# Preparing the next pair's rows in DRAM during the second scan, and putting the stores of the last result between the convolution's rows

## The chip, the cores and the metric

The kernel runs on one core of a Trainium2 chip. The metric is the device time of one execution in microseconds (us); smaller is better. Engine names in the profile are PE (TensorE, with PEld for its weight loads), DVE (VectorE), ACT (ScalarE), POOL (GpSimd) and SP (the engine whose queue issues most transfers). An engine's name with a q (SPq, ACTq) is its sequencer, which issues transfers and waits.

## The reference, cut to what matters

Eight images of 64 channels and 128 x 128 pixels pass through four residual layers in float32:

```python
x = x + _L0_conv_ref(_gn(x), ...)   # deformable convolution, batch norm over all images, relu
x = x + _L1_conv_ref(_gn(x), ...)   # 3x3 convolution
x = x + _L2_conv_ref(_gn(x), ...)   # state-space scan over rows and over columns, mixed by a linear map
x = x + _L3_conv_ref(_gn(x), ...)   # quarter-size image, nearest neighbours, attention, upsampling
```

`_gn` is a group norm: it needs the mean and variance over a whole image of two channels each. The batch norm at the end of layer 0 needs statistics over all eight images, so that layer 0 is finished for every image before its result can be scaled, put through the relu and added to x.

## The kernel before, in words

Two images make a pair, with 2 x 64 channels on the 128 partitions; four pairs are worked through. The deformable layer (the first 14 ms) leaves its raw result of each pair in DRAM, in `self.y[p]`. Everything after it is in `rest`. Two buffers of the size of an image pair, `rooms[0]` and `rooms[1]`, stay in SBUF, and change roles with each pair: `now` (called `a`) holds the running sum x, `other` (called `b`, or `two` in the convolution) holds an intermediate.

For each pair p:

- `conv3x3` scales x by the group norm (`nx`, L574, sixteen steps of 8 rows) and sends each step by four transfers from SP (L576, L577) into `two`, a copy of the image split in even and odd rows. TensorE then multiplies (L588), and VectorE adds into `a` (L590). Between its steps, the nearest-neighbour stage of the pair before (`neighbours`, the generator `aside`) is advanced. That stage begins with `quarter`, which reads `self.y[p]` back from DRAM by transfers from ACT (L1036) and multiplies it (L1022, L1044).
- `scan_layer` normalizes a into b (`first_norm`), and runs two ways, over rows and over columns. A way has a pass back and a pass ahead of 16 blocks each (`NG` is 16). In a round of the pass ahead (`Scan.ahead`) the inputs of a block two rounds on are read from `b` (L1224) and rearranged by transfers from SP (L1226, tile `in`), the states of the pass back are loaded (L1280, tile `zb`), POOL adds and multiplies (L1242, L1286, L1288, L1334), VectorE scans (L1257), TensorE mixes (L1235, L1302, L1320, L1338), and VectorE adds to `a` (L1340). In the second way it also takes statistics of `a` (L1343), two instructions a block. Each round ends with `next(aside)`. The first way's `aside` is the second way's pass back; the second way's `aside` is `following`.
- `following` prepares pair p + 1. It does nothing for `NG - 1` rounds. Then, when `b` is no longer read, it calls `finish_deform`: sixteen chunks of 1024 columns, each with a load of x into `b` (L540), a load of y into a small buffer (L542), the batch norm and relu on ACT (L543), the addition by POOL and VectorE in turn (L544) and two statistics on VectorE (L546). The small buffers are three that stand free: the tiles `inb` and `fx` of the scan, and a slot of `tabs`.
- After `scan_layer`, sixteen stores from SP (L504) write the finished `a` to `self.y[p]`. They are ahead of the next convolution's row transfers in the same queue, and those overwrite the same SBUF buffer.

The code's order is a priority and not the order on the chip: the order of the instructions on each engine is settled when the program is built, and in the profile some instructions of a later step stand well ahead of their place in the code. On the chip each engine runs its list in order and waits at semaphores.

Of the kernel before, what the change touches and what calls it, by code (L numbers as in the profile page):

```python
# [9 lines left out]
F32 = mybir.dt.float32  # L10
I32 = mybir.dt.int32
AF = mybir.ActivationFunctionType
# [4 lines left out]
P = 128  # L17
# [3 lines left out]
CH = 512  # L21
NCH = HW // CH
# [6 lines left out]
NB = 256  # L29
NG = HW // (T * NB)  # L30
# [11 lines left out]
class Net:  # L42
# [434 lines left out]
    def rest(self):  # L477
        tc, nc = self.tc, self.nc
        with ExitStack() as ctx:
            pool = lambda name, bufs, **kw: ctx.enter_context(tc.tile_pool(name=name, bufs=bufs, **kw))  # L480
            self.big = pool("b_big", 1)
            self.small = pool("b_small", 2)
            self.tables = pool("b_tables", 2)
            self.ps = pool("b_ps", 2, space=PSUM)
            self.ps1 = pool("b_ps1", 1, space=PSUM)
            self.back = [[self.dram.tile([P, 2, NB], F32, name=f"back{d}_{g}") for g in range(NG)] for d in range(2)]
            rooms = [self.big.tile([P, ROOM], F32, name=f"room{k}") for k in range(2)]
            image = lambda t: t[:, 0:HW].rearrange("p (h w) -> p h w", h=H)
            aside = iter(())
            with tc.tile_pool(name="b_first", bufs=6) as wp:  # L490
                first = self.finish_deform(0, image(rooms[0]), lambda n: wp.tile([P, 1024], F32, tag="y", name=f"yr0_{n}"))
                for _ in first:
                    pass
            for p in range(self.npair):
                now, other = rooms[p % 2], rooms[(p + 1) % 2]
                a, b = image(now), image(other)
                r, nb = self.conv3x3(p, a, other, *self.gn1, aside)
                norm = self.scan_layer(p, a, b, r, nb)
                af = now[:, 0:HW]

                for n in range(8):
                    for half in range(2):
                        s = slice((half * 8 + n) * 1024, (half * 8 + n + 1) * 1024)
                        nc.sync.dma_start(self.y[p][:, s], af[:, s])  # L504
                aside = self.neighbours(p, self.y[p] if p + 1 < self.npair else af, norm)
            for _ in aside:
                pass

    def setup_deform(self, psum):

# [36 lines left out]
            yield  # L547
        self.gn1 = self.groupnorm(self.small, self.ps1, "small", st, "gn1")

    def conv3x3(self, p, a, room, r, nb, aside):  # L550

# [7 lines left out]
        with self.tc.tile_pool(name=f"b_conv{p}", bufs=1) as cp, self.tc.tile_pool(name=f"b_conv2_{p}", bufs=2) as wp:  # L559
# [3 lines left out]
            for e in range(2):  # L563
                for n in range(2):
                    for h in range(2):
                        dy = 2 * n - 1 + h - e
                        if abs(dy) < 2:
                            nc.scalar.dma_start(w[half[h], e, n], src[:, 3 * dy + 3 : 3 * dy + 6, :])
            nc.gpsimd.memset(two[half[0], :, 0, :], 0.0)
            nc.gpsimd.memset(two[half[1], :, H // 2, :], 0.0)  # L570
            for n in range(16):
                t = wp.tile([P, 2, 4, H], F32, tag="t", name=f"nx{p}_{n}")
                rows = a[:, 8 * n : 8 * n + 8, :].rearrange("p (m e) w -> p e m w", e=2)
                nc.scalar.activation(t, rows, AF.Identity, bias=nb, scale=r)  # L574
                for i in range(2):
                    nc.sync.dma_start(two[half[1], i, 4 * n : 4 * n + 4, :], t[half[i], 0])  # L576
                    nc.sync.dma_start(two[half[0], i, 4 * n + 1 : 4 * n + 5, :], t[half[i], 1])  # L577
            for n in range(0, H // 2, 4):
                for e in range(2):
                    po = self.ps.tile([P, 4, H], F32, tag="b", name=f"c1_{p}_{n}_{e}")  # L580
# [337 lines left out]
    def scan_layer(self, p, a, b, r, nb):  # L918
# [3 lines left out]
        with tc.tile_pool(name=f"b_scan{p}", bufs=2) as wp:  # L922
            ways = [Scan(self, wp, p, d, a, b, st) for d in range(2)]

            back = ways[0].back("in", "z", "h")
            for _ in self.first_norm(wp, p, a, b, r, nb):
                next(back)
                next(back)
            for _ in back:
                pass  # L930
            ways[0].ahead(ways[1].back("inb", "zbk", "fx"))

            def following():

                rooms = [(wp, "inb", [P, 2, 2, NB]), (wp, "fx", [P, 2, 2, NB]), (self.tables, "tabs", [P, NSTATE])]

                def room(n):
                    pool, tag, shape = rooms[n % 3]
                    kind = {"bufs": 1} if pool is wp else {}
                    t = pool.tile(shape, F32, tag=tag, name=f"yr{p + 1}_{n}", **kind)  # L940
                    return t[:, 0:1024] if len(shape) == 2 else t.rearrange("p i h m -> p (i h m)")

                for _ in range(NG - 1):
                    yield
                for n, _ in enumerate(self.finish_deform(p + 1, b, room)):
# [477 lines left out]
```

## Time and profile before

| | us |
|---|---|
| median of three runs (18770.06 to 18828.75) | 18815.32 |
| the profiled execution, its own time | 18647.43 |
| its span in the profile | 18645.6 |
| the deformable layer, up to the first load L540 | 13996.8 |
| the last addition to `a` (L1340) of pairs 0, 1 and 2 ends | 15061.0, 16187.2, 17315.4 |
| the convolution (L588) of pairs 1, 2 and 3 starts | 15103.6, 16229.3, 17357.6 |
| that convolution ends | 15352.0, 16476.4, 17605.6 |

| engine | busy us | share of the span |
|---|---|---|
| PE | 11123.6 | 60% |
| DVE | 11377.5 | 61% |
| POOL | 11000.0 | 59% |
| ACT | 3024.1 | 16% |

The shares are means over stages that differ much. What is of use is the busy time in a short stretch, the waits in it, and the instructions in order of time. The profiled execution was faster than the three runs; a saving found in the profile is therefore taken as a difference, not as a time. Positions such as 15061.0 are microseconds from the span's start.

### The profile page before, as it was taken

To read this page: it belongs to the slowest core of one execution; us is meant where nothing else is said; L and a number is where in the kernel's file an instruction comes from. 1 tells how busy PE (TensorE), PEld (TensorE's weight loads), DVE (VectorE), ACT (ScalarE), POOL (GpSimd) and SP (SyncE) were. 2 spreads that over 40 slices of the span, in tenths; PEclk is the share of its full clock that TensorE was granted. 3 is DMA by queue.
4 is the path that set the end of the run, shared out by engine and by line. 5 is a ranking of instruction groups with operands and counts; after the bars stand their busy time and mean duration, and the time that the engine had idled before them with its cause. 6 is when DMAs were issued, how large, how long until landed. Compare 5 with 4: busy or idle time off the path is not lost. (4 is left out here: it accounts for less than half of the span.)

```text
span 18645.6 us, 118301 instructions
## 1 busy us (share of the span) xinstructions
PE 11123.6 (60%) x31224; PEld 3929.2 (21%) x31224; DVE 11377.5 (61%) x27180; ACT 3024.1 (16%) x5658; POOL 11000.0 (59%) x10484
## 2 busy tenths in 40 slices
PE   6655455545555554445654555555427988889886
PEld 1111111111111111111111111111102434435343
DVE  5566666556665556656665566555664765667566
ACT  1000111001100000010000000000003425334242
POOL 5766766666666666766666676766671413315142
PEclk8777677767777666777776777667658989999898
DMA  4333333333333333333333333333333243422423
GB/s 150 103 100 104 116 113 116 109 112 111 117 111 98 97 94 113 112 113 110 100 95 100 93 99 99 99 96 93 92 92 94 69 144 79 130 87 70 142 76 101
DMA packets 900049, 1933.33 MB, mean 104 GB/s; under 512 B 199852, under 2 KB 435764, under 8 KB 876340
## 3 DMA queue, kind: packets, MB, share of 16 engines
q0 software_dynamic: 442368, 1208.55, 21.7%
q1 hardware_dynamic: 381968, 679.49, 11.9%
q10 hardware_dynamic: 75044, 37.72, 1.0%
q8 instruction: 255, 4.18, 0.1%
q14 instruction: 414, 3.39, 0.1%
HBM read 1540.72 MB, written 208.10 MB: 94 GB/s over the span
## 5 line engine op out<-in xcount | busy, mean ns | idle before, releaser
L371 POOL DMA_INDIRECT g<-table,idx x9216 | 9526.3, 1034 | 4333.7 <-issue 2626.2
L381 DVE TENSOR_REDUCE sm<-g 128x64 f32<-128x256 f32 x9216 | 5062.9, 580 | 3356.0 <-remote 2479.9
L289 PE MATMUL po<-xe,wt 128*54 128x512 f32 (+3 forms) x8384 | 4668.4, 666 | 534.0 <-ACT ob L299 390.9
L380 DVE TENSOR_TENSOR g<-g,wts 128x256 f32<-128x256 f32 x9216 | 3561.8, 415 | 552.9 <-DMA g<-table,idx 488.5
L387 PE MATMUL sp<-ident,sm 128*128 128x128 f32 x4096 | 1494.5, 375 | 3632.2 <-DVE sm L381 1853.0
L390 ACT COPY s<-sp 128x512 f32<-128x512 f32 x1024 | 598.1, 584 | 9537.5 <-remote 3918.3
L387 PEld LDWEIGHTS sp<-ident,sm 128*128 128x128 f32 x4096 | 619.5, 155 | 6387.2 <-DVE sm L381 2381.4
L395 PE MATMUL yp<-s,wd 128*64 128x512 f32 (+1 forms) x2560 | 933.0, 736 | 1367.3 <-ACT s L390 756.3
L289 PEld LDWEIGHTS po<-xe,wt 128*54 128x54 f32 x8384 | 916.4, 138 | 1863.7 <-issue 1192.8
L872 POOL COPY l_yb<-ln_y 128x512 f32<-128x512 f32 x128 | 72.8, 612 | 1295.9 <-DVE ln_y L121 1295.9
L588 PE MATMUL c<-room,l_w 128*64 128x508 f32 (+1 forms) x3072 | 741.8, 597 | 22.2 <-DMA room<-nx 16.1
L1242 POOL TENSOR_TENSOR u<-u,v 128x512 f32<-128x512 f32 x256 | 327.9, 1281 | 680.0 <-DVE v L1241 548.8
L1224 ACT ACTIVATE fx<-room,ln_b,ln_g 128x512 f32<-128x512 f32 x512 | 639.2, 1292 | 169.9 <-DMA in<-fx 148.1
L1334 POOL TENSOR_TENSOR ms<-ms,ln_y 128x512 f32<-128x512 f32 x256 | 274.0, 1090 | 640.2 <-DVE ln_y L121 600.3
L389 PE MATMUL s<-ident,sm 128*64 128x128 f32 x1024 | 343.5, 335 | 449.7 <-DVE sm L381 151.2
L396 DVE BATCH_NORM_STATS2 ystat<-yp 128x6 f32<-128x512 f32 x128 | 89.3, 697 | 844.2 <-PE yp L395 498.7
L395 PEld LDWEIGHTS yp<-s,wd 128*64 128x64 f32 (+1 forms) x2560 | 222.9, 161 | 1810.2 <-issue 1000.3
L1257 DVE TENSOR_TENSOR_SCAN z<-tabs,z,u 128x256 f32<-128x256 f32 x512 | 435.4, 876 | 214.8 <-POOL u L1242 186.2
L1235 PE MATMUL pv<-in,tabs 128*128 128x512 f32 x1024 | 506.4, 617 | 41.9 <-DVE u L1241 40.0
L1320 PE MATMUL pc<-outs,h 128*128 128x256 f32 x2048 | 497.7, 386 | 28.0 <-DVE h L1305 25.8
L1302 PE MATMUL py<-x,outs 128*128 128x512 f32 x1024 | 507.3, 599 | 6.8 <-POOL x L1288 6.4
L1302 PE MATMUL py<-in,outs 128*128 128x512 f32 x1024 | 507.3, 608 | 1.7 <-ACT h L1304 1.0
(414 smaller groups left out, 10197.6 us busy)
## 6 DMA issues: line engine op xcount, KB each, us to landing
g<-table,idx POOLq DMA_INDIRECT x9216
in<-fx SPq DMA_DIRECT2D x1024, 128.0 KB
xe<-in_x_dram SPq DMA_DIRECT2D x56, 1408.0 KB
table<-q SPq DMA_DIRECT2D x256, 256.0 KB
y<-ys SPq DMA_DIRECT2D x128, 256.0 KB
room<-in_x_dram SPq DMA_DIRECT2D x64, 512.0 KB
yr<-y SPq DMA_DIRECT2D x64, 512.0 KB
room<-nx SPq DMA_DIRECT2D x256, 128.0 KB
```

Of the source, the lines that this page charges most:

```text
L289: nc.tensor.matmul(po[:, r0:r1, c0:c1], lhsT=wt[:, t, :], rhs=xe[:, row + r0 : row + r1, c0 + dx : c1 + dx], start=n == 0, stop=n == len(u ...
L371: nc.gpsimd.indirect_dma_start(out=tq[:, k, :], out_offset=None, in_=flat[i], in_offset=bass.IndirectOffsetOnAxis(ap=idx[:, at : at + 1], ...
L380: nc.vector.tensor_mul(t[:, k], t[:, k], w)
L381: nc.vector.tensor_reduce(sm[:, k], t[:, k].rearrange("p q c -> p c q"), axis=mybir.AxisListType.X, op=ALU.add)
L387: nc.tensor.transpose(sp[:, j, :], sm[:, j * P : (j + 1) * P], self.ident)
L390: nc.scalar.copy(st[i][:, 0:4, m * P : (m + 1) * P], sp)
L395: nc.tensor.matmul(yp[i * C : (i + 1) * C, :], lhsT=wd[0:rows, j, :], rhs=st[i][0:rows, j, :], start=j == 0, stop=j == 4)
L588: nc.tensor.matmul(o, lhsT=lt, rhs=mv, start=k < 2, stop=k >= len(calls) - 2)
L1224: nc.scalar.activation(fx[:, e].rearrange("p h (o m) -> p h o m", m=self.INNER), src[:, e::2], AF.Identity, bias=w["ln1_b"], scale=w["ln1_g"])
L1235: nc.tensor.matmul(pv, lhsT=tabs[:, at : at + P], rhs=fx[:, :, h, :], start=h == 0, stop=h == 1)
L1302: nc.tensor.matmul(py, lhsT=lt, rhs=mv, start=n == 0, stop=n == len(calls) - 1)
L1320: nc.tensor.matmul(pc[:, i], lhsT=hs[:, h, i, m * P : (m + 1) * P], rhs=self.outs[:, CEN : MIX + P], start=True, stop=True)
```

## The change

`following` now starts at the first round of the second way ahead. It takes one buffer for x (`inb`) and one for y (the slot of `tabs`), and a new function, `prepare_deform`, does in each round one chunk: load x, load y, relu on ACT, addition on POOL (all sixteen), two statistics on VectorE, and a store of the sum to `self.y[p + 1]` in DRAM. The sixteenth chunk and the group norm's few steps follow in round sixteen. Then eight loads of 2048 columns (1 MB each) bring the finished rows from DRAM into `b`. The stores of pair p's result are a generator, `stores`, which `conv3x3` advances: two steps (four stores of 512 KB) ahead of its row steps, and one step (two stores) after every second row step.

```diff
-                r, nb = self.conv3x3(p, a, other, *self.gn1, aside)
+                r, nb = self.conv3x3(p, a, other, *self.gn1, stores, aside)
                 norm = self.scan_layer(p, a, b, r, nb)
                 af = now[:, 0:HW]
-
-                for n in range(8):
-                    for half in range(2):
-                        s = slice((half * 8 + n) * 1024, (half * 8 + n + 1) * 1024)
-                        nc.sync.dma_start(self.y[p][:, s], af[:, s])
+                stores = self.stores(p, af)
                 aside = self.neighbours(p, self.y[p] if p + 1 < self.npair else af, norm)
+            for _ in stores:
+                pass
...
+    def stores(self, p, af):
+
+        for n in range(8):
+            for half in range(2):
+                s = slice((half * 8 + n) * 1024, (half * 8 + n + 1) * 1024)
+                self.nc.sync.dma_start(self.y[p][:, s], af[:, s])
+            yield
...
+    def prepare_deform(self, p, xr, yr):
+
+        nc = self.nc
+        st = self.small.tile([P, NCH, 6], F32, tag="st", name=f"gn1_st{p}")
+        for n in range(16):
+            s = slice(n * 1024, (n + 1) * 1024)
+            nc.sync.dma_start(xr, self.x[p * P : (p + 1) * P, s])
+            nc.sync.dma_start(yr, self.y[p][:, s])
+            nc.scalar.activation(yr, yr, AF.Relu, bias=self.bn0_bias, scale=self.bn0_scale)
+            nc.gpsimd.tensor_add(xr, xr, yr)
+            for m in range(2):
+                nc.vector.bn_stats(st[:, 2 * n + m, :], xr[:, m * CH : (m + 1) * CH])
+            nc.sync.dma_start(self.y[p][:, s], xr)
+            yield
+        self.gn1 = self.groupnorm(self.small, self.ps1, "small", st, "gn1")
...
+            for _ in range(2):
+                next(stores, None)
             nc.gpsimd.memset(two[half[0], :, 0, :], 0.0)
             nc.gpsimd.memset(two[half[1], :, H // 2, :], 0.0)
             for n in range(16):
...
+                if n % 2:
+                    next(stores, None)
...
-                rooms = [(wp, "inb", [P, 2, 2, NB]), (wp, "fx", [P, 2, 2, NB]), (self.tables, "tabs", [P, NSTATE])]
-
-                def room(n):
-                    pool, tag, shape = rooms[n % 3]
-                    kind = {"bufs": 1} if pool is wp else {}
-                    t = pool.tile(shape, F32, tag=tag, name=f"yr{p + 1}_{n}", **kind)
-                    return t[:, 0:1024] if len(shape) == 2 else t.rearrange("p i h m -> p (i h m)")
-
+                xr = wp.tile([P, 2, 2, NB], F32, tag="inb", name=f"xr{p + 1}", bufs=1).rearrange("p i h m -> p (i h m)")
+                yr = self.tables.tile([P, NSTATE], F32, tag="tabs", name=f"yr{p + 1}")[:, 0:1024]
+                made = self.prepare_deform(p + 1, xr, yr)
                 for _ in range(NG - 1):
+                    next(made, None)
                     yield
-                for n, _ in enumerate(self.finish_deform(p + 1, b, room)):
-                    if n % 4 == 3:
+                for _ in made:
+                    pass
+
+                bf = b.rearrange("p h w -> p (h w)")
+                for n in range(8):
+                    s = slice(n * 2048, (n + 1) * 2048)
+                    nc.sync.dma_start(bf[:, s], self.y[p + 1][:, s])
+                    if n % 3 == 2:
                         yield
```

`finish_deform` stays, for the first pair alone.

More of the change, by code (lines that the diff above doesn't have):

```diff
@@ L488, in rest @@
             image = lambda t: t[:, 0:HW].rearrange("p (h w) -> p h w", h=H)
-            aside = iter(())
+            aside, stores = iter(()), iter(())
             with tc.tile_pool(name="b_first", bufs=6) as wp:
@@ L548, in finish_deform, with conv3x3 @@
         self.gn1 = self.groupnorm(self.small, self.ps1, "small", st, "gn1")
-    def conv3x3(self, p, a, room, r, nb, aside):
+    def prepare_deform(self, p, xr, yr):
[12 more added lines that the diff above has]
+        self.gn1 = self.groupnorm(self.small, self.ps1, "small", st, "gn1")
+    def conv3x3(self, p, a, room, r, nb, stores, aside):
         nc, src = self.nc, self.ins["l1_w"]
```

## The prediction

> **What bounds the kernel now.** I read the page's 40 slices first (the first 30 are the deformable layer, which the change doesn't touch), then busy time by stretch for one joint between two pairs of images, then who waited for whom there, then the instructions in order. The change acts at the three joints between the four pairs. The last pair has no successor, so its second way ahead shows that stage without the preparation: the two can be held against each other. Columns of the first view: stretch, its length, then busy us (and count) of PE, PEld, DVE, ACT, POOL; granted clock, DMA share, GB/s.
>
> ```profile
> 14800.00:14975.00 175.00, 174.89 (x580) 99.51 (x579) 155.73 (x329) 77.02 (x156) 96.56 (x77) 1.00 0.20 50
> 14975.00:15029.00 54.00, 41.15 (x110) 21.86 (x108) 47.26 (x74) 18.18 (x33) 32.13 (x19) 0.87 0.64 218
> 15029.00:15063.00 34.00, 9.19 (x34) 6.16 (x34) 32.32 (x60) 9.99 (x15) 16.22 (x10) 0.62 0.54 189
> 15063.00:15104.00 41.00, 13.44 (x103) 10.84 (x104) 7.16 (x48) 2.83 (x3) 0.61 (x2) 0.58 1.03 308
> 18186.00:18361.00 175.00, 174.94 (x581) 99.70 (x580) 155.81 (x327) 76.34 (x155) 96.86 (x78) 1.00 0.20 50
> 18361.00:18395.00 34.00, 33.75 (x110) 18.79 (x109) 30.25 (x62) 8.98 (x24) 17.54 (x15) 1.00 0.10 24
> 18395.00:18413.00 18.00, 6.71 (x32) 4.75 (x30) 11.30 (x26) 3.08 (x9) 6.08 (x6) 0.72 0.02 7
> ```
>
> Lines 1 and 5 are the steady part of the second way, first and last pair: TensorE is full, and a round takes 15.7 us (distance of the L1343 statistics in the trace). VectorE has 155.73 of 175, 89%, or 14.0 us a round. Then the pairs part: the rest takes 54 + 34 us in the first pair and 34 + 18 in the last. From the first L1343 to the last it is 259.2, 259.2, 257.9 us in pairs 0 to 2 and 224.2 in pair 3. **35 us a joint** are thus what `finish_deform` costs where it stands, and there VectorE is the bound (47.26 of 54, 32.32 of 34) while TensorE starves. Line 4 is the joint's second loss: 41 us in which hardly an engine works and DMA is full.
>
> ```profile
> 15061.02 25.72 SPq L504 DMA_DIRECT2D y<-room  x16
> 15084.31 0.67 PE L1044 MATMUL pd<-yq,l_wr 128*64 128x128 f32 x2 [7.24 <-DMA yq<-y]
> 15088.26 0.47 SPq L576 DMA_DIRECT2D room<-nx  x1
> 15096.25 0.46 SPq L577 DMA_DIRECT2D room<-nx  x1
> 15103.59 3.94 PE L588 MATMUL c<-room,l_w 128*64 128x512 f32 x6 [3.36 <-DMA room<-nx]
> ```
>
> Sixteen stores occupy SP for 25.72 us, 1.6 us each; the convolution's rows (L576, L577) come behind them, and beside both run the quarter image's loads (yq). The convolution starts 40.6 us after the last statistics (40.0 and 40.1 at the other joints). In the first pair, with no stores, it starts 4.9 us after `nx` (14051.4 to 14056.3). Once started it is TensorE-bound: 245.45 us busy of 248.
>
> **What the Trainium skill says.** "SBUF — State Buffer", Who interferes with whom: a VectorE instruction with two SBUF inputs contends with a GpSimd instruction that reads SBUF; one blocks for the other's whole length. The trace agrees: the two scans below (0.74 us each alone) take 4.41 beside one L544 addition on POOL.
>
> ```profile
> 14982.11 2.33 POOL L544 TENSOR_TENSOR room<-room,yr 128x1024 f32<-128x1024 f32 x1
> 14982.18 4.41 DVE L1257 TENSOR_TENSOR_SCAN z<-tabs,z,u 128x256 f32<-128x256 f32 x2 [0.53 <-POOL u L1242]
> ```
>
> "GPSIMD Engine Reference", Engine selection: two-input elementwise work is about twice as slow there; here 2.35 against 1.21 us for L544. "DMA: Bandwidth & Descriptors", Issuing engines are not separate DMA queues: transfers issued from SP and ACT share the same 16 engines; line 4 above, with share 1.03 while both issue, fits. Same page, Two DMAs through the same engine are not ordered: a dependent transfer must wait for the first one's completion, so a row of `two` waits for the store that empties its place; the border fill on POOL started at 15065.98, released by the first store, 5.0 us after its issue.
>
> **The change, part by part (per joint; three joints).**
>
> 1. *Taken out of the tail:* 16 relus, 16 additions, 32 statistics. Gain: the measured difference, 35.0 us, if nothing takes its place. What is late next there is TensorE, as in pair 3.
>
> 2. *Put into the rounds:* one chunk a round, 15 rounds. VectorE: 2 x 0.68 = 1.37 us, 14.0 to 15.3, still under 15.7. All 16 additions now go to POOL (half did before): 2.35, which takes POOL from 8.7 to 11.0. ACT: 1.24, 6.9 to 8.2. SP: two loads and a store at 0.33. DMA: 1.5 MB, at the 2.5 us per MB of the first pair's loads 3.8 us a round, on top of a share of 0.20. None of these is full; on paper the cover (TensorE at 15.7) holds. But about 4.9 of VectorE's 14 us are two-input operations (two scans 1.48, two L1305 1.36, twelve small ones 2.1), so I estimate that a 2.35 us addition blocks one some two times in three for half its length: 0.75. VectorE then needs 16.1, 0.4 above TensorE. Queueing at such loads costs more; the trace shows no round of this mix. Bounds: 0 (all hidden; below nothing is excluded, since TensorE was already full) and +2 a round (every addition blocks for nearly all its length and something queues behind). I take +0.7: 15 x 0.7 = **11 us lost**.
>
>  The new waits are on SP, which is in order. In the steady rounds it already waits most of the time for the `zb` buffer:
>
> ```profile
> SPq L1280 <- PE zt L1282: 146.3, 14, 12.4
> ```
>
>  Behind a store that waits for POOL, or a load that waits for the store before it (one `xr`, one `yr`), stand `in<-fx` (whose reader is TensorE's L1235) and `zb<-back`. A chunk's chain is 5 us for the store to be known as landed (as above), as much for the loads (an estimate), 1.24 and 2.35: 13.6 of 15.7. It fits in a round, with 2 us to spare; that is the weak place.
>
> 3. *At the end of the way:* eight 1 MB loads of ready rows, 20 us at 2.5 us per MB, from the last read of `b` (before, L540 began at 14974.9). `in` and `zb` of the last round are issued at 14989.6 and 14992.1, inside that stretch; the transfer ahead can make them up to 8 us late, none if they go first. I take **5 lost**. The rows are in place by about 15005, 60 us ahead of `nx`.
>
> 4. *Stores between rows:* of 16 stores, 4 go ahead (6.4 us of SP), then 8 row transfers at 0.55 (4.4 us) and 3.6 us from row to convolution as in the first pair: start some 14 us after the last addition to `a`, against 42: 28 gained. But TensorE now does 9.7 us of the quarter image's products (L1022, L1044) in that gap; they move into a stage where it is 99% busy. That leaves 18. The second chunk of the quarter image (at 15094.89, ahead of the convolution on TensorE) reads y that is now stored only after the second and fourth row step; if it keeps its place, the convolution queues behind it. I take **15 gained**, bounds 0 and 25. The additional 8 MB written and 8 MB read per joint are those of 2 and 3.
>
> Costed at nothing: the smaller set of buffers (their own waits are in 2), the first pair (`stores` is empty there), the last pair (its stores and nearest-neighbour stage follow as before), GroupNorm's statistics (same number, now early; about 8 us of small VectorE steps leave the joint, inside the 41 us of which 4 already counts).
>
> Sum per joint: 35 - 11 - 5 + 15 = 34; three: **102 us**. Against the profiled execution (span 18645.6, 1.8 us around it, 18647.4) that gives 18545. The median of the three runs is 18815.3, 0.9% above that execution, and I take the same saving off it: **18713**.
>
> **Rivals.**
>
> - *All hidden:* rounds stay at 15.7 (2 us lost in all), the head gains 25: 58 a joint, 174, 18641. For it: VectorE's sum of 15.3 is under TensorE's. Against: the blocked scans shown above.
> - *Eaten up:* rounds reach +2, 30 us: 35 - 30 - 5 + 15 = 15 a joint, 45, 18770, or the chunks are queued so late that the tail stays much as it was. Against the latter: in the trace before, the first two L543 ran at 14743.97, some 245 us ahead of the others, so the order of instructions lets ready work go early.
> - *Slower:* the chunk chain overruns its round, and SP, held by a store or by a load that waits for a store, gives `in<-fx` late, so that TensorE stops in every round. The decision falls at +3.0 us a round (35 - 5 + 15 = 45, over 15). At +4.5, with a head gain of 10: 35 - 67 - 5 + 10 = -27, times three 81 slower, 18896. For it: 13.6 of 15.7 in a chain over four in-order queues. Against: SP's waits for `zb` are slack, up to 12.4 us a round, and inputs are asked for two rounds ahead.
>
> **How the numbers follow.** Main case 0.48, all hidden 0.18, eaten up 0.18, slower 0.16. A measurement of this kernel can tell about 0.3% (56 us) from no change. Faster by more: most of the main case (0.45), all of the second, a sixth of the third (0.03): 0.66. Within: the rest of those two, 0.18. Slower: 0.16. The range runs from 18600 (all hidden, and 40 for the spread of the runs, 18770 to 18829) to 18860, which leaves out only the far part of the slower case.
>
> **What would show it.** Right: the distance of L1343 within 16.0 to 17.0 us in the rounds; the end of the way at 16, 14, 11 and 9 us as in pair 3, with a few us more; VectorE at 95% or more in the rounds; the convolution 15 to 30 us after the last statistics. Wrong: TensorE waiting for `in<-fx` in the rounds (slower), rounds at 15.7 (all hidden), the tail still at 20 us and more a round, or the convolution still 40 us late because L1044 or the rows wait for stores.

## The result, and the profile after

The changed kernel takes **18865.22 us** (median of 15 runs, 18812.55 to 18968.35) against 18799.39 us of the kernel before, run beside it (15 runs, 18726.26 to 18867.85). The ratio is **1.0039, interval 1.0025 to 1.0052**: 66 to 73 us slower, where 102 us were forecast to be saved. The forecast of 18713 was wrong in direction, and the time lies 5 us above the stated range.

The profiled execution has a span of 18810.8 us, 165 more than before. Of these, 105 lie in the deformable layer, which the change doesn't touch: the first `nx` starts at 14156.7 instead of 14051.4. From there to the end it is 4654.1 against 4594.2 us, **60 us more**. So I compare only stages after the first `nx`:

| us (pairs 0, 1, 2) | before | after |
|---|---|---|
| lead-in: first norm to the first statistic of the second way ahead | 572.1, 563.4, 568.5 | 589.3, 578.1, 586.5 |
| first to last of those statistics | 259.3, 259.1, 257.9 | 263.0, 264.1, 260.6 |
| last statistics to the convolution's start | 40.5, 40.1, 40.2 | 9.7, 9.4, 9.8 |
| length of the convolution | 248.4, 247.0, 248.0 | 265.3, 264.0, 267.4 |
| convolution's end to the next first norm | 14.7, 14.7, 14.7 | 28.5, 29.0, 28.6 |
| sum of the last three rows | 303.7, 301.8, 302.8 | 303.5, 302.4, 305.8 |

The first two rows lose 61 us in all; the joint, taken as a whole, stays as it was within 3 us. Pair 3 gains 9 in its lead-in, though nothing is prepared there: lead-ins without preparation lie between 560 and 572 us in the kernels of this document, so that is scatter. In pair 0 they are 571.9 to 572.2 us in four kernels, and below I compare by pair 0.

First the busy time by stretch of the changed kernel (columns as in the prediction): six rounds with chunks, the rounds after them, the end of the way, the stretch after it, joint, convolution, gap.

```profile
14926.90:15054.90 128.00, 107.77 (x316) 59.05 (x314) 104.99 (x199) 51.39 (x95) 75.95 (x52) 0.92 0.51 161
15054.90:15125.40 70.50, 67.75 (x220) 38.42 (x220) 58.31 (x123) 29.00 (x61) 39.60 (x32) 0.98 0.18 49
15125.40:15172.70 47.30, 43.66 (x148) 24.59 (x147) 40.57 (x102) 14.03 (x34) 21.98 (x19) 1.00 0.59 218
15172.70:15191.00 18.30, 5.85 (x27) 3.86 (x25) 11.88 (x27) 3.51 (x9) 5.89 (x6) 0.64 0.07 28
15190.10:15199.80 9.70, 1.14 (x4) 1.00 (x4) 4.66 (x24) 1.24 (x1) 0.94 (x4) 0.50 0.85 296
15199.80:15465.00 265.20, 255.06 (x1302) 114.78 (x1302) 127.72 (x300) 48.04 (x89) 0.00 (x0) 0.98 0.50 136
15465.00:15493.60 28.60, 1.89 (x9) 1.54 (x7) 23.36 (x62) 2.00 (x6) 0.00 (x0) 0.55 0.56 222
```

Read line 1. By the statistics the first six rounds take 17.7, 20.3, 22.8, 24.3, 17.8 and 20.9 us (the stretch is 4 us longer than they are), 20.6 in the mean instead of 15.7. TensorE works in 107.77 of 128 us at a granted clock of 0.92, and VectorE only in 104.99, 82%. No engine is full, and yet the round is a third longer. Lines 3 and 4 are the tail: its last four rounds take 16.0, 17.9, 11.5 and 9.3 us (before 25.1, 23.0, 21.8, 15.0). The last two lines are the joint: a convolution at TensorE's limit, then 28.6 us in which TensorE does next to nothing.

What was waited for in that stretch (us in total, times, longest):

```profile
PE pc L1348 <- DVE h L1333: 15.2, 6, 4.0
DVE gn_st L567 <- POOL xr L565: 7.6, 7, 1.6
ACT yr L564 <- DMA yr<-y: 21.6, 8, 6.2
SPq L568 <- POOL xr L565: 39.3, 8, 8.9
```

TensorE waits for `h`, which VectorE adds; among its waits there is none for `in<-fx`. SP does wait for POOL ahead of its stores (line 4), as foreseen, and ACT for the load of its chunk (line 3), but neither TensorE nor VectorE waits for a transfer. The relu starts nine times in these 128 us: chunks come every 12.6 us, from ahead of the first statistic of the way (L564 at 14849.1) to 15037.6, and the sixteenth is over in the sixth round.

The joint in the order of time: the last addition to `a` is followed by the rows and the convolution with hardly a pause, and the quarter image's products (L1072, `pd`) come in the middle of it.

```profile
15188.79 4.23 SPq L512 DMA_DIRECT2D y<-room  x4
15195.69 0.47 SPq L600 DMA_DIRECT2D room<-nx  x1
15197.36 0.47 SPq L601 DMA_DIRECT2D room<-nx  x1
15199.83 4.45 PE L614 MATMUL c<-room,l_w 128*64 128x512 f32 x6 [6.70 <-DMA room<-nx]
15216.94 3.98 PE L1072 MATMUL pd<-yq,l_wr 128*64 128x128 f32 x32
15493.10 0.29 DVE L910 TENSOR_SCALAR center_r<-center,gn_y 128x128 f32<-128x128 f32 x1 [4.01 <-DMA out_dram<-up_x]
15493.60 3.75 PE L928 MATMUL pc<-room,center_r 128*128 128x512 f32 x4 [8.69 <-DVE z L1281]
```

The last two lines say what ends the gap: the first norm's weights (`center_r`) on VectorE wait for the transfer `out_dram<-up_x`. That is the last store of the nearest-neighbour stage, not the convolution. (The last line names `z`, which VectorE runs 0.3 us after `center_r`.)

### The profile page after: what moved, and what is told of

The parts are those of the page before. It is cut to its first block, busy times and chain, and to the rows that moved or that the text cites. A ratio compares the mean times of both kernels' runs of the same rounds, so it can differ in the third digit from the quotient of the medians.

```text
span 18810.8 us, 118433 instructions
## 1 busy us (share of the span) xinstructions
PE 11052.5 (59%) x31224; PEld 3934.1 (21%) x31224; DVE 11326.2 (60%) x27156; ACT 3020.9 (16%) x5658; POOL 11152.6 (59%) x10508
## 5 line engine op out<-in xcount | busy, mean ns | idle before, releaser
L371 POOL DMA_INDIRECT g<-table,idx x9216 | 9634.8, 1045 | 4316.0 <-issue 2636.4
L289 PE MATMUL po<-xe,wt 128*54 128x512 f32 (+3 forms) x8384 | 4621.8, 660 | 725.4 <-ACT ob L299 495.0
```

Source lines behind the costliest of these rows:

```text
L289: nc.tensor.matmul(po[:, r0:r1, c0:c1], lhsT=wt[:, t, :], rhs=xe[:, row + r0 : row + r1, c0 + dx : c1 + dx], start=n == 0, stop=n == len(u ...
L371: nc.gpsimd.indirect_dma_start(out=tq[:, k, :], out_offset=None, in_=flat[i], in_offset=bass.IndirectOffsetOnAxis(ap=idx[:, at : at + 1], ...
```

## The experiments

The kernel before takes about 16450 us on three of the chips used for the experiments and about 18800 us on two. The traces put the difference into the deformable layer, which all these kernels share: the first `nx` starts at 11.84 to 11.87 ms on the former and at 14.16 to 14.28 ms on the latter. Every ratio is taken on one chip. Lengths of stages are compared between traces of both kinds, whose rounds without preparation take 15.7 us alike. "Way and lead-in" is the sum of the first two rows of the table for pair 0: 831.4 us before, 852.3 with the change, and 792.9 in pair 3 of the kernel before, which prepares nothing. Theory A, formed from the lines above: a chunk's arithmetic lengthens the chain of a round, which runs over several engines. Rivals: the transfers and SP's waits; the bunching of chunks ahead of time; POOL blocking VectorE.

**The two halves of the change.** The preparation alone has the stores drained ahead of the convolution:

```diff
+                for _ in stores:
+                    pass
                 r, nb = self.conv3x3(p, a, other, *self.gn1, stores, aside)
```

> The preparation alone; all sixteen stores ahead of the convolution as before. Theory A (the rounds of the second way lose more than the tail gains, and the joint is set by the nearest-neighbour stage, so that the stores' new place gives nothing): early rounds of 18 to 24 us and a tail of 16, 18, 11.5, 9 as in the whole change, some 22 us a joint lost, 60 to 75 us slower than before in all (1.003 to 1.004). Theory B (the stores between the rows cost the time, the preparation is worth its tail): faster than before by 50 us or more.

Measured: 16516.43 against 16449.24, ratio 1.0038 (1.0024 to 1.0053); way and lead-in 855.5; joint 302 us. The stores alone have the old `following`:

```diff
-                made = self.prepare_deform(p + 1, xr, yr)
...
+                for n, _ in enumerate(self.finish_deform(p + 1, b, room)):
```

> The stores between the rows alone; the next pair's rows made at the end of the second way as before. Theory A: the convolution starts some 30 us earlier, takes some 17 us longer and is followed by a gap some 14 us longer, because the quarter image's loads wait for the later stores and the nearest-neighbour stage ends when it did; total within 20 us of before (1.000). The prediction's step 4: 15 us a joint, 45 us faster (0.9976). Theory B: slower by 60 us or more.

Measured: ratio 1.0001 (0.9992 to 1.001); way and lead-in 832.7; convolution 11 us after the last statistics, 265 to 267 us long, then a gap of 29; sum of the joint 306 to 308. Both came out as theory A had it. So the whole loss is the preparation's, and the stores between the rows bring nothing: what their early convolution gains is given back as a longer convolution and a longer gap.

**Transfers or arithmetic.** One kernel moves the chunks and computes nothing on them (it leaves out relu, addition and statistics), the other computes on the first chunk over and over and moves only the first in and the last out:

```diff
-            nc.scalar.activation(yr, yr, AF.Relu, ...)
-            nc.gpsimd.tensor_add(xr, xr, yr)
-            for m in range(2):
-                nc.vector.bn_stats(...)
```

> The whole change without the relu, addition and statistics of the prepared chunks (the loads and stores stay; the group norm's statistics of pairs 1 to 3 are a constant, so its output is not the reference's). Theory C or P (engines held by the chunk's compute, by waiting or by blocking): rounds back at 15.7 to 16.2, end of the way as in the last pair with a few us more. Theory D (the transfers themselves and the store and load waits on SP make the scan's own inputs late): rounds stay at 18 us and more, TensorE waiting for in<-fx.

> The whole change, but only the first chunk is loaded and only the last stored: the relu, addition and statistics of sixteen chunks run on resident data (its output is not the reference's). Theory P (blocking of VectorE by POOL, and the engines' added load): rounds stay long, 18 us and more while chunks run, though the chunks may run faster than one per 12 us and so be over sooner. Theory C (waits of in-order engines for the chunk's loads): the rounds fall to 16 to 17 us, the total lost over the way below 15 us.

Transfers only: one run of 16373.98 (before 16449.24), way and lead-in 806.8, rounds 16.4, 15.7, 15.7, 15.5, 17.7 and then 15.7. Arithmetic only: 16467.42 (before 16452.83), way and lead-in 836.6; its sixteen chunks, which no transfer holds back, came 5.5 us apart within 90 us, all ahead of the first statistic of the way. Above the 792.9 of pair 3, all the loads and stores together stand at 14 us and the arithmetic alone at 44, where the whole change stands at 59. The arithmetic is thus three quarters of it, and the transfers with SP's waits are the smaller part.

**Other shapes of the chunk.** All additions on VectorE instead of POOL; chunks of 512 columns in two pairs of half buffers; and the whole change with the statistics left out. The first of these edits:

```diff
-            nc.gpsimd.tensor_add(xr, xr, yr)
+            nc.vector.tensor_add(xr, xr, yr)
```

> The whole change, but all sixteen additions on VectorE (about 1.21 us each in place of 2.35 on POOL). Theory P (POOL's additions block VectorE's two-input operations, some 12 us of excess per 195 us in the trace): the early rounds fall by about a third of their excess, some 12 us a joint, so 35 us faster than the whole change. Theory C (the chunk's chain over one pair of buffers makes ACT wait for its load, 33 us of 186, and whatever is behind it): rounds stay at 18 to 24 us, within 15 us of the whole change, or longer as VectorE carries 1.21 us more.

> The whole change with chunks of 512 columns in two pairs of half buffers (same SBUF), so that one half's transfers run under the other's compute, and POOL's additions are half as long. Theory C: waits of ACT for yr fall from 33 us per 186 to 10 or less, and the rounds to 16 to 17: 25 us a joint less than the whole change, so 75 us faster than it and about level with before. Theory P: the same blocked time in more pieces, rounds still 18 us and more.

> The whole change without the statistics of the prepared chunks (a constant takes their place, so its output is not the reference's); relu, POOL's additions and all transfers stay. If VectorE's 22 us of statistics a joint are what doesn't fit: way and lead-in fall by 22 us or more from the whole change's 46 over the transfers alone. If POOL's blocking and the waits for loads are: they fall by less than 10 us.

Ratios 1.0023 (1.0015 to 1.0031) and 1.0021 (1.0015 to 1.0028); one run of 18794.8 (before 18803.75) without statistics, in which the stages from the first `nx` to the end still take 4636.2 us, 42 more than before. Way and lead-in 843.5, 842.6 and 843.7. Each takes some 9 of the 21 us back, and none of them removes the cost. The halves still have rounds of 19.5 to 22.2 us while chunks run, where 16 to 17 were forecast; the fall without statistics stays under the 10 us forecast for waits and blocking; and the additions on VectorE, 26 us faster than the change by the ratios, lie between their two forecasts. POOL's blocking can be seen, but is small:

```profile
14991.81 2.35 POOL L565 TENSOR_TENSOR xr<-xr,yr 128x1024 f32<-128x1024 f32 x1
14991.89 4.42 DVE L1285 TENSOR_TENSOR_SCAN z<-tabs,z,u 128x256 f32<-128x256 f32 x2 [1.16 <-POOL u L1270]
```

In this timeline of the changed kernel the two scans (0.74 us each alone) take 4.42 beside one addition, which agrees with the Trainium skill, "SBUF — State Buffer", Who interferes with whom. Over the 195 us with chunks (14850 to 15045), VectorE's instructions that overlap L565 are about 14 us longer in all than the same ones elsewhere in that stretch, an estimate from the means of each kind. That is 0.9 us a chunk, of the 3.2 that a chunk costs.

**Bunching.** Theory B: chunks come every 12.6 us and not every round; one a round would cost what was forecast. To hold them back, the relu's bias is made from a value of the round before:

```diff
+            bias = self.bn0_bias
+            if self.pace is not None:
+                bias = self.small.tile([P, 1], F32, tag="pace", ...)
+                nc.vector.scalar_tensor_tensor(bias, self.pace[:, 0:1], 0.0, self.bn0_bias, ALU.mult, ALU.add)
-            nc.scalar.activation(yr, yr, AF.Relu, bias=self.bn0_bias, scale=self.bn0_scale)
+            nc.scalar.activation(yr, yr, AF.Relu, bias=bias, scale=self.bn0_scale)
...
+            self.net.pace = made[2] if made else None
```

> The whole change, but the relu of a chunk takes its bias from a one-column copy that depends on the LayerNorm factor of the round just ended, so that chunks run one a round and cannot gather at the way's start. Theory G (gathering: chunks run every 12.6 us and not one a round, so VectorE's work passes the round of 15.7 us in the first half of the way, while the slack of the later rounds is not used): rounds of 16 to 17 us throughout, the way and its lead-in together some 15 us over the last pair's in place of 46; some 90 us faster than the whole change, some 25 to 50 us faster than before. Theory W (each chunk costs its 3 us wherever it stands, by waits in the in-order queues): the same loss spread over 15 rounds, 18 to 19 us each, level with the whole change.

Measured: ratio 1.0075 (1.0048 to 1.0102), rounds steady at 20.3 us, way and lead-in 873.0. Theory B falls: one chunk a round costs 4.6 us, and in the change, where chunks come faster, one costs less (51 us over 16 chunks, 3.2 each).

**One operation a round.** The paced form allows the price of each part to be measured: relu, addition and two statistics together on resident data, then each kind alone (the transfers and the other parts are left out). A small VectorE instruction of 0.16 us a round, the same in all four, holds the chunk back until the round before has made its value.

```diff
+            if self.pace is not None:
+                nc.vector.scalar_tensor_tensor(yr[:, 0:1], self.pace[:, 0:1], 0.0, self.bn0_bias, ALU.mult, ALU.add)
```

> One chunk's relu, addition and statistics in each round of the second way, started by that round's LayerNorm factor, on resident data without the loads and stores (the output is not the reference's). Theory R (the round is a closed chain over VectorE, POOL, TensorE and ACT, and an instruction put into it on any of them lengthens it, though no engine is full): rounds of 19 to 20.3 us, near the 20.3 of the paced whole change. Theory T (the loads and stores and SP's waits make the difference): 16 to 17 us.

> As before, POOL's addition alone, one a round (2.35 us; the output is not the reference's). Theory R with POOL as the chief part: 17.5 to 18.5 us a round (2.35 less what POOL idled before its next link). If POOL's 45% idle time takes it: 15.7.

> ACT's relu alone, one a round (1.24 us; the output is not the reference's). Theory R: up to 17 us. If ACT's 56% idle time takes it: 15.7.

> VectorE's two statistics alone, two a round (1.37 us, on resident data; the output is not the reference's). Theory R: 16.5 to 17.1 us. If VectorE's 1.7 us of idle time a round takes them, as the prediction's step 2 had it: 15.7 to 15.9.

Six steady rounds of each, same columns. The kernel before:

```profile
14819.50:14914.10 94.60, 94.52 (x313) 53.78 (x312) 84.10 (x176) 41.44 (x84) 52.81 (x43) 1.00 0.21 51
```

with a relu a round (16378.88 us in one run, way and lead-in 802.4):

```profile
12633.60:12728.60 95.00, 94.50 (x313) 53.63 (x312) 84.23 (x181) 48.57 (x90) 53.80 (x43) 1.00 0.20 50
```

with an addition on POOL a round (16432.1 us, 824.4):

```profile
12622.50:12724.60 102.10, 96.59 (x313) 53.05 (x312) 84.85 (x182) 40.94 (x85) 67.97 (x49) 1.00 0.19 47
```

with the statistics alone on VectorE (16439.62 us, 826.0), and below it the statistics of chunks in these six rounds:

```profile
12618.00:12723.10 105.10, 96.01 (x314) 53.29 (x313) 92.03 (x187) 41.45 (x84) 51.82 (x42) 1.00 0.19 45
```

```profile
L569 DVE BATCH_NORM_STATS2 gn_st<-yr x6: 694/694/694, 12632.6 to 12720.2; 128x6 f32<-128x512 f32 x6
```

That is one statistic a round and not the two that were planned. The pacing instruction writes the first column of `yr`; the second statistic reads the other half of `yr`, waits for nothing, and in this kernel ran ahead of the rounds (all sixteen stand before 12564, ahead of the way's first statistic).


with all of them (16558.6 us, 869.6; the kernel before took 16451.74):

```profile
12644.20:12766.20 122.00, 106.02 (x313) 59.04 (x313) 95.22 (x194) 49.01 (x90) 65.40 (x49) 0.92 0.16 39
```

A sixth of the length, less 15.7, is the price of each in a round: relu 0.1, addition 1.3, one statistic 1.8, all together (with two statistics) 4.6. The relu's kernel also clears the pacing instruction and the smaller set of buffers, which it shares with the others. The last one, without a transfer, has the round of the paced whole change (20.3): there the arithmetic is all of it. In the statistics' kernel VectorE works 92.03 over 6, 15.3 us a round, and TensorE needs 15.7; the round takes 17.5. So a round is not the largest of its engines' sums. Of the forecasts, that for all together held; the addition came out below its range, and one statistic above the range for two.

Where the time goes is seen in the waits. With the addition alone VectorE's scan waits for `u`, which now stands behind the addition in POOL's list (the line isn't there in the kernel before):

```profile
DVE z L1287 <- POOL u L1272: 7.0, 6, 1.2
```

With the statistics, the order of VectorE's list is another: one of the two additions to `h` stands ahead of the two scans in the kernel before, and in the three paced kernels with statistics shown so far both stand behind them. Before:

```profile
14852.73 1.36 DVE L1305 TENSOR_TENSOR h<-h,in 128x512 f32<-128x512 f32 x1
14854.02 2.40 DVE L1257 TENSOR_TENSOR_SCAN z<-tabs,z,u 128x256 f32<-128x256 f32 x2
14856.34 0.66 DVE L1305 TENSOR_TENSOR h<-h,in 128x512 f32<-128x512 f32 x1
```

With one statistic a round:

```profile
12637.00 2.39 DVE L1288 TENSOR_TENSOR_SCAN z<-tabs,z,u 128x256 f32<-128x256 f32 x2 [0.19 <-POOL u L1273]
12639.31 2.33 DVE L1336 TENSOR_TENSOR h<-h,in 128x512 f32<-128x512 f32 x2
```

In this kernel the statistic of a chunk stands between the additions to `h` of one round and the scans of the next; what the additions now stand behind is the scans. The group of TensorE's `pc` shows the result. Its columns are busy us and mean ns, then the idle time before it and what ended it. In the kernel before, with a transposing product of the same stretch below it:

```profile
L1320 PE MATMUL pc<-outs,h 128*128 128x256 f32 x96 | 22.7, 379 | 0.0
L1282 PE MATMUL zt<-z,turn 128*128 128x512 f32 x12 | 6.1, 592 | 0.0
```

With one statistic a round:

```profile
L1351 PE MATMUL pc<-outs,h 128*128 128x256 f32 x96 | 23.3, 386 | 9.1 <-DVE h L1336 9.1
```

With all three:

```profile
L1353 PE MATMUL pc<-outs,h 128*128 128x256 f32 x96 | 29.5, 462 | 16.0 <-DVE h L1338 16.0
L1315 PE MATMUL zt<-z,turn 128*128 128x512 f32 x12 | 10.4, 968 | 0.0
```

The 27.4 us that all the arithmetic adds to six rounds are, on TensorE, 16.0 of waiting for `h` and 11.5 of longer matmuls. The microseconds of one round (granted clock in the third column from the end) show why these are longer:

```profile
12648.00:12649.00 1.00, 0.48 (x2) 0.00 (x0) 1.00 (x2) 0.26 (x1) 1.00 (x2) 1.00 0.00 0
12650.00:12651.00 1.00, 0.00 (x0) 0.00 (x0) 1.00 (x2) 0.00 (x0) 0.33 (x1) 1.00 0.47 145
12652.00:12653.00 1.00, 1.00 (x4) 0.73 (x4) 1.00 (x2) 0.14 (x1) 0.21 (x1) 0.50 0.00 0
12654.00:12655.00 1.00, 1.00 (x3) 0.51 (x2) 0.08 (x1) 0.50 (x2) 0.77 (x1) 0.50 0.93 207
12655.00:12656.00 1.00, 1.00 (x5) 0.62 (x4) 0.81 (x2) 0.15 (x1) 0.00 (x0) 0.97 0.86 201
```

After 2.7 us of standing still the array gets half its clock for some 3.4 us. The Trainium skill, "TensorE: Matmul & The Clock Gate", Part 1: The HAM clock gate, describes an activity window of about 3.4 us that runs freely, and half rate after an idle window. The 3.4 us at half clock fit that length, but the pause is shorter than a whole window, so less than the page asks for was enough here. After the 1.5 us of the statistics' kernel the clock stays at 1.00.

**Is the clock part of the cost?** It looked as if it were 1.9 of the 4.6 us (11.5 over 6). To test it, two, three and six matmuls that nobody reads fill the idle stretch, in the paced arithmetic; and six in the whole change:

```diff
+                if self.d and self.p + 1 < net.npair and h == m == 0:
+                    for i in range(6):
+                        nc.tensor.matmul(pc[:, i % 2], lhsT=net.turn, rhs=self.outs[:, CEN : MIX + P], start=True, stop=True)
```

> The kernel of the paced arithmetic (one relu, one addition and two statistics a round on resident data, no transfers; its statistics are not those of the data), with six matmuls of 128x256 written into pc ahead of the ones that wait for h; the first real matmul overwrites what they leave. They fill about 1.4 us of the 2.7 us in which TensorE stood idle in each round, so that the array does not stand still so long. Theory (clock): of the 4.6 us that the paced arithmetic cost a round, 1.9 are TensorE at half its clock after the idle stretch (pc at 462 ns in the mean and zt from z at 968 instead of 379 and 592). Filled, both go back to 379 and 592, the granted clock to 0.99 or 1.00, and a round takes 18.3 to 18.8 us. Rival (chain only): the round is set by VectorE and POOL, and a slow TensorE is no part of it: the matmuls get shorter, the wait for h gets longer, and the round stays at 20.0 to 20.3 us.

> The whole change, with the same six matmuls ahead of the waiting pc in the second way of the first three pairs. Theory (clock): of the 51 us that pair 0 lost in lead-in and first eleven rounds, about 15 are TensorE at a lower clock after its idle stretches (granted 0.92 in six rounds). Most of it comes back, less 1.4 us in each round that had no idle stretch: lead-in and way of pair 0 about 840 to 845 us instead of 852.3, three pairs 20 to 36 us, ratio to the kernel before 1.0020 to 1.0030 instead of 1.0039. Rival (chain only): the filler brings nothing or costs: 852 us or more, ratio 1.0039 or higher.

> The paced arithmetic with two matmuls of 128x256 instead of six ahead of the waiting pc (computation altered as before). From the run with six, whose filler took 2.75 us, two take 0.92 us of the 2.67 us of idle time, and leave 1.7. Theory (clock): the array's clock stays at or near 1.00, pc at 379 to 390 ns, zt from z at 592, and a round takes 18.3 to 18.8 us. Rival (chain only): the round stays within 20.0 to 20.7, whatever the clock, and the slow matmuls are replaced by waiting. If the clock still falls, the run tells nothing but that 1.7 us is enough for it.

> The same with three matmuls: 1.37 us of filler, 1.3 us of idle time left, less than the 1.5 us at which the clock stayed at 1.00 with the statistics alone. Theory (clock): granted clock 1.00, a round of 18.3 to 18.8 us. Rival (chain only): clock 1.00 and the round at 20.0 to 21.4 us, with the time now waited out at pc, pv or pt.

I had the fillers at half their length: six took 2.75 us, the whole idle stretch. Rounds of pair 0: two fillers 19.5 to 21.3 us at a clock of 0.95; three 20.4 at 1.00; six 21.4 at 1.00. Single runs: 18963.12 and 18981.02 (before 18792.26) and 16649.31 (before 16449.13). The whole change with six fillers was much worse, 16714.71 us, ratio 1.0163 (1.0149 to 1.0177). Five rounds with three fillers, and what TensorE waits for there:

```profile
15013.00:15115.00 102.00, 86.95 (x290) 49.72 (x289) 65.89 (x159) 38.43 (x75) 55.39 (x40) 1.00 0.14 39
```

```profile
L1268 PE MATMUL pv<-in,tabs 128*128 128x512 f32 x20 | 9.8, 611 | 14.3 <-DMA in<-fx 14.3
```

The clock is full and no `pc` waits; VectorE needs 65.89 over 5, 13.2 us, a sixth less than the 15.9 without fillers (its scans take 0.75 us in the mean instead of 1.23, its additions to `h` 0.69 instead of 1.20); and the round is as long as ever, with 2.9 us of waiting now at `pv`. My clock theory fails: with the fillers in, the full clock came with no shorter round. But the fillers also changed the order of TensorE's list (`pv` stands elsewhere) and of VectorE's (both additions to `h` stand between the scans with three fillers, ahead of them with six), so these runs don't isolate the clock, and whether it would count with the old order is open.

**Where the joint's gain went.** In the kernel with the stores alone, the quarter image is read from the input x instead of the stored y, so that its loads wait for no store (for three pairs the stage then computes on other data):

```diff
+            src = self.x[p * P : (p + 1) * P, :] if p + 1 < self.npair else src
```

> The stores between the rows alone (as in the run of that change), with the quarter image of pairs 0 to 2 read from the kernel's input and not from the stored result, so that its loads need not wait for the stores (its output is not the reference's). Theory Q (the nearest-neighbour stage, started by these loads, sets when the next scan can begin): the time from the last statistics to the next first norm falls from 306 us to 285 us or less, the convolution's end and the neighbours' end draw together. Rival (TensorE's work or the row transfers set it): it stays at 302 to 308.

Joint 290.3, 290.8 and 291.4 us instead of 306, from the first `nx` to the end 4557.2 us against 4594.2 before (one run; its whole time, 18834.88, differs in the deformable layer). The forecast of 285 or less was missed by 5. The quarter products, by source line (first and last start), before:

```profile
L1044 PE MATMUL pd<-yq,l_wr x256: 388/407/476, 15084.3 to 15168.2; 128*64 128x128 f32 x128
```

after:

```profile
L1072 PE MATMUL pd<-yq,l_wr x256: 386/405/422, 15216.9 to 15310.1; 128*64 128x128 f32 x128
```

with the quarter from x (its last statistics end at 15287.9):

```profile
L1071 PE MATMUL pd<-yq,l_wr x256: 386/405/424, 15317.6 to 15389.1; 128*64 128x128 f32 x128
```

From the end of the last statistics (15063.0 before, 15190.1 after) the last product starts 105 us later before, 120 after, 101 here. The end of the neighbours' stage (the last up-sampling instruction) is 296.2, 299.0 and 285.8 us after them, and the next first norm follows it by 4.5 to 7.5 us in all three. The convolution ends at 288.9, 275.0 and 275.9. So the end of the neighbours' chain sets the joint, and freeing its loads from the stores shortens the joint: a convolution that starts 30 us earlier ends 14 earlier and then waits.

**A better place.** If the second way has no room, the convolution may: after the change POOL has 0.00 and ACT 48.04 of its 265.20 us. In the last kernel the next pair is prepared between the convolution's row steps, in halves of 512 columns; the loads stay at the end of the second way, the stores go ahead of the rows as before.

```diff
+        if p + 1 < self.npair:
+            xr, yr = (self.tables.tile([P, NSTATE], F32, tag="tabs", ...)[:, 0:1024] for k in "xy")
+            made = self.prepare_deform(p + 1, xr, yr)
...
                     next(aside, None)
+                    next(made, None)
```

> The preparation moved out of the scan into the convolution of the pair before, where POOL is idle, ACT 20% and VectorE 55% busy; half chunks, in the two slots of tabs; loads of ready rows at the end of the second way as in the change; all stores ahead as before. If the rounds are where the change loses and the tail where it gains, the second way runs as in the last pair with some 5 us more: 30 us a joint gained, 90 us faster than before (0.995), less what the convolution stage loses. The rival: the nearest-neighbour stage, which sets that stage's end, is made later by as much as the preparation's 22 us of VectorE a joint: total within 40 us of before.

Measured: 16407.99 against 16452.83, **ratio 0.9974 (0.9963 to 0.9985): faster than both kernels**, 45 us by the medians, between the main forecast of 90 and the rival's 40. The rounds of the second way are full again, and in the convolution of pair 1 TensorE works 246 of 260 us:

```profile
12608.00:12784.00 176.00, 175.47 (x581) 99.53 (x580) 156.56 (x334) 76.74 (x155) 96.53 (x77) 1.00 0.20 50
12883.00:13143.00 260.00, 245.99 (x1203) 108.24 (x1202) 150.34 (x334) 67.64 (x118) 35.54 (x24) 0.99 0.66 187
```

Way and lead-in of the three pairs take 803.1, 801.3 and 787.1 instead of 831.4, 822.5 and 826.4: 89 us gained. The first convolution grows from 167 to 185.5 us, and the next two joints to 320.5 and 323.1: 57 us given back. From the first `nx` to the end the traces have 4564.4 us against 4594.2 before, 30 less; where the other 15 of the 45 come from isn't shown. The neighbours' stage of the two joints ends 315 and 317 us after the last statistics, so I take it to be what makes them late; that wasn't tried.

## Why the prediction was wrong

1. *Taken out of the tail, 35 us.* Right. The last four rounds took 84.9 us and take 54.7: 30.2 gained, which is 35 less the 5 of step 3.

2. *Put into the rounds, 0.7 us each, 11 lost.* **This step failed: its model of a round was wrong, and the term mis-sized with it.** Lead-in and the first eleven rounds of pair 0 lost 17.2 + 34.1 = 51 us, 3.2 a chunk. VectorE's need was forecast about right, 16.1 us a round against 15.9 with all the arithmetic, but in part by luck. The blocking, put at 0.75 a round, was about that in the change, 0.9 a chunk; in the paced rounds the addition alone left VectorE at 84.85 us over six rounds, 84.10 before and 1.0 of pacing. The 15.9 hold instead 0.4 of longer additions to `h` and 0.2 of pacing. The error was the inference: that a round costs the largest of the sums, 16.1 at most, and that "on paper the cover holds". Before, the lists were so ordered that TensorE waited for nothing, and of VectorE's 1.7 idle us a round 1.1 were a wait for POOL's `x`. What is put into VectorE's and POOL's lists comes ahead of `u` or `h`, which others wait for, or changes the order in which these are made, and the idle time is not used up: on VectorE it is 2.2 us a round with one statistic and 4.5 with all. The upper bound of 2 a round came from blocking and what queues behind it, so it left this out. That chunks would come one a round was wrong too: they came every 12.6 us, and paced to one a round they cost 4.6 each.

3. *Loads at the end, 5 lost.* Consistent: the last four rounds stand 54.7 to the 49.8 of pair 3 before.

4. *Stores between rows, 15 gained a joint.* **Failed.** The convolution started even sooner than forecast (9.7 us against 14), and the quarter products did move into it: it is 17 us longer. But the sum ended at the convolution. The next first norm waits for the end of the neighbours' stage, whose first loads now wait for later stores. The lower bound of 0 was the measured value; the text had named the quarter image as what could turn the gain to nothing, for another reason (the place in TensorE's list).

The sum at the joint was to be 35 - 11 - 5 + 15 = 34; it was 35 - 51 - 5 + 0 = -21, three of them -63, and the runs show 66 to 73 lost.

*The rivals.* The slower case came near the right total (81 us slower) with the wrong mechanism. Its decision point of +3.0 us a round was passed at 3.2, and with nothing gained at the head it falls to 1.9 a chunk (35 - 5 over 16). But TensorE never waited for `in<-fx` in the change's measured rounds, with transfers alone most rounds stay near 15.7, and the paced rounds take 20.3 us with the transfers and SP's waits and without. "VectorE at 95% or more in the rounds" was the sign asked for; 82% was seen, the clearest mark in the profile that the model of the round, and not a price, was at fault.

What stays open: how much of the price of a statistic is the order of the list and how much its own length, which no run holds apart; how the 1.4 us by which all the arithmetic exceeds the sum of its measured parts divides among the second statistic, list order and the lower clock; and why the rounds of the kernels without statistics and with additions on VectorE vary between 16 and 28 us.

## What to carry to other kernels

In a stage like this, where one engine is full and the others wait for each other in every round, don't take another engine's idle share for room: insert one such instruction a round and measure what it costs before summing busy times, and look where it lands in the list relative to what others wait for. Put added work where an engine has nothing to do for a whole stage, as POOL in the convolution here. And when a transfer is moved to start a stage sooner, find first which chain releases the stage after it, and whether that chain reads what the moved transfer writes.

## What the runs showed of the hardware that I had not expected

A relu of 1.24 us on ACT in each round costs 0.1 us, an addition of 2.35 us on POOL 1.3, and one statistic of 0.69 us on VectorE (with 0.16 of pacing) 1.8, twice their own length. A pause of TensorE of 2.7 us was followed by 3.4 us at a clock of 0.50 in the rounds of the paced arithmetic; pauses of 1.5 us were not, and neither was one of 2.7 us in the kernel with three fillers (15042.56 to 15045.30, clock 1.00 throughout). The length of a pause alone does not decide it. One and the same program, the kernel before, took about 16450 us on some chips and about 18800 us on others.
